# Layer 1 takes turned memories from layer 0 through DRAM, with the normalisation folded into weights and one scaling

## The chip, the cores and the metric

The kernel runs on one core of one Trainium2 chip. The time is the device time of one execution in microseconds. The engines are TensorE (PE; PEld for its weight loads), VectorE (DVE), ScalarE (ACT), GpSimd (POOL) and SyncE (SP); DMAs are issued from SP, ACT and POOL.

## The reference, cut to what matters

Two layers of a Perceiver work on latents `x` (16 batches of 64 rows of 256) and on one memory `ctx` (16 batches of 1601 rows of 256). Both layers attend to the same memory. Layer 0 attends to the raw memory with 32 chosen keys, layer 1 to its layernorm with 16 heads:

```
x = x + L0_xattn(layernorm(x), ctx, top_k=32)     # scores = q . (ctx Wk + bk), 32 largest kept
x = x + L0_attn(layernorm(x))                     # retention
x = x + L0_ffn(layernorm(x))                      # an attention over positions, then 8 experts
x = x + L1_xattn(layernorm(x), ctx, ctx)          # see below
x = x + L1_attn(layernorm(x)); x = x + L1_ffn(layernorm(x))

def L1_xattn(q, k, v):
    mu, var = mean(k), var(k)                      # over the 256 features of a memory row
    kn = (k - mu) * rsqrt(var + 1e-5) * norm_w + norm_b      # the same for v, and for q
    Q, K, V = qn @ Wq + bq, kn @ Wk + bk, kn @ Wv + bv       # 16 heads of 16
    out = softmax(0.25 * Q K^T) V + Q
    return layernorm(out, norm1_w, norm1_b) @ Wo + bo + out
```

## The kernel before

All data is fp32. A memory of 1601 rows is held with rows on the partitions as 13 chunks of 128 rows (the last of 65). To multiply it by weights or queries it has to be turned, features on the partitions: `mT`, 128 partitions by 2 halves of the features by 1601 columns. TensorE turns one 128x128 block at a time against an identity.

**Layer 0** (lines 225 to 394) works on pairs of memories, eight pairs. `turned_pair` loads two memories with SP (lines 215, 218; six buffers, so three pairs), turns them (line 248) and copies the blocks from PSUM to `mT` with ACT (line 253; two buffers, so one pair). `scored_pair` multiplies them by the queries (line 290), `choose` finds the 32 largest scores with DVE (lines 312 to 322), and `gather`, two pairs behind, turns the weights and multiplies them by the unturned memory (lines 333, 346). The turned memories are dropped after the scores.

**Retention, position attention and experts** follow (lines 515 to 896). The framework orders the instructions of each engine here by a model of its own: an instruction that is ready by that model is put ahead of program order. So work of layer 1 stands between instructions of these stages.

**Layer 1's memory attention** loads every memory again. `fetch` is `load_mem` and `normalise`: DVE takes mean and variance of each row (`bn_stats`, `bn_aggr`, lines 415 and 416), ACT a square root, DVE its reciprocal, and POOL subtracts and scales in place (line 426). `turned_mem` turns the normalised memory with TensorE (line 439) and ACT copies it out with `norm_w` and `norm_b` (line 444). `keys` (line 460, copied out by ACT at 468) and `values` (line 482, copied out by DVE at 490) multiply it by the weights `wk` and `wv`.

Memories 0 and 1 are prepared ahead of the loop (lines 899 to 909); the keys and values of memory 0 too. Then a loop runs over 128 units: 16 batches by 4 parts of the columns by 2 halves of the heads. In a unit, TensorE makes scores (981), DVE their maxima (995), ACT the exponents (997); the exponents of the unit before are turned (1010), copied out (1015, 1017) and multiplied by the values (1029). Between these, one step at a time, stand the keys and values of memory b+1, the turning of memory b+2 (`next(turns)`, eight steps in eight units) and the statistics of memory b+3 (`next(norms)`, four steps a unit from the fourth unit on). `collect` joins the parts of batch b-1 in units 1 to 3. In this loop the order of TensorE, VectorE and ScalarE is written by hand, that is, it is program order:

```python
order = {mybir.EngineType.PE, mybir.EngineType.DVE, mybir.EngineType.Activation}
with tc.manual_schedule(engines=order):
    for u in range(len(units) + 1):
```

POOL and SP keep the order of the framework's model. Weight matrices are loaded by `load_square`, here on POOL's queue.

Of the kernel before, what the change touches and what calls it, by code (L numbers as in the profile page):

```python
# [31 lines left out]
KEY_STEPS = ((1, 0), (3, 0), (3, 1), (1, 1), (2, 0), (2, 1), (0, 0), (0, 1))  # L32
TURN_STEPS = ((3, 0), (3, 1), (1, 0), (1, 1), (2, 0), (2, 1), (0, 0), (0, 1))
VALUE_STEPS = (2, 1, 1, 2, 2, 2, 2, 1)
# [31 lines left out]
def perceiver_kernel(  # L66
# [154 lines left out]
    def chunk(c):  # L221
        return P if c < 12 else TAIL


    with ExitStack() as ph:
# [11 lines left out]
        def turned_pair(k, mems, memTs):  # L237

            for h in range(2):
                mems.append(load_mem(memp, 2 * k + h))  # L240
                memTs.append(work.tile([P, 2, S], F32, name="mT", tag="mT"))
            for n0, n in SCH:
                for h in range(2):
                    for dc in range(2):
                        pt = ps_m.tile([P, 512], F32, name="pt", tag="mm")
                        for j in range((n + P - 1) // P):
                            c = n0 // P + j
                            nc.tensor.transpose(  # L248
                                pt[:, j * P : j * P + chunk(c)],
                                mems[h][0 : chunk(c), c, dc * P : (dc + 1) * P],  # L250
                                ident[0 : chunk(c), 0 : chunk(c)],
                            )
                        nc.scalar.copy(memTs[h][:, dc, n0 : n0 + n], pt[:, 0:n])  # L253
                        yield

# [143 lines left out]
    x1 = ctx.enter_context(ExitStack())  # L399
    wp = x1.enter_context(tc.tile_pool(name="x1_w", bufs=1))  # L400
# [4 lines left out]
    w_x = load_square(wp, w_x1, 4, "w_x")  # L405
    wq, wk, wv, wo = (w_x[:, i, :, :] for i in range(4))

    def normalise(mt):

        st = small.tile([P, NC, 6], F32, name="m_st", tag="m_st")  # L410
        mv = small.tile([P, NC, 2], F32, name="m_mv", tag="m_mv")
        nc.gpsimd.memset(mv[:, 12, :], 1.0)
        for c in range(NC):
            m = chunk(c)
            nc.vector.bn_stats(out=st[0:m, c, :], in_=mt[0:m, c, :])  # L415
            nc.vector.bn_aggr(out=mv[0:m, c, :], in_=st[0:m, c, :])
            yield
        sd = small.tile([P, NC], F32, name="m_sd", tag="m_sd")
        nc.scalar.activation(sd, mv[:, :, 1], AF.Sqrt, bias=eps)
        rstd = small.tile([P, NC], F32, name="m_rstd", tag="m_rstd")  # L420
        nc.vector.reciprocal(rstd, sd)
        nmean = small.tile([P, NC], F32, name="m_nmean", tag="m_nmean")
        nc.gpsimd.tensor_scalar(nmean, mv[:, :, 0], -1.0, None, ALU.mult)
        for c in range(NC):
            m = chunk(c)
            nc.gpsimd.tensor_scalar(  # L426
                mt[0:m, c, :], mt[0:m, c, :], nmean[0:m, c : c + 1], rstd[0:m, c : c + 1],
                ALU.add, ALU.mult,
            )
            yield  # L430

    def turned_mem(mt, mT, pool):

        for part, dc in TURN_STEPS:
            c0, nch, n = PARTS[part]
            pt = pool.tile([P, 512], F32, name="pt", tag="mm")
            for j in range(nch):
                c = c0 + j
                nc.tensor.transpose(  # L439
                    pt[:, j * P : j * P + chunk(c)],  # L440
                    mt[0 : chunk(c), c, dc * P : (dc + 1) * P],
                    ident[0 : chunk(c), 0 : chunk(c)],
                )
            nc.scalar.activation(  # L444
                mT[:, dc, c0 * P : c0 * P + n], pt[:, 0:n], AF.Identity,
                bias=col("L1_norm_b", dc), scale=col("L1_norm_w", dc),
            )
            yield

# [3 lines left out]
    def keys(mT, kT, pool):  # L453

        for part, oc in KEY_STEPS:
# [3 lines left out]
            for dc in range(2):  # L459
# [8 lines left out]
            nc.scalar.activation(  # L468
                kT[:, oc, n0 : n0 + n], ps[:, 0:n], AF.Identity, bias=col("L1_bk", oc)
            )  # L470
# [30 lines left out]

    mems, mTs, kvs, kvs_of = {}, {}, {}, {}

    def fetch(b):
        mems[b] = load_mem(memp, b)
        return normalise(mems[b])

    def run(steps):
        for _ in steps:
            pass  # L510

# [3 lines left out]
    with ExitStack() as ph:  # L515
# [383 lines left out]
    for b in range(2):  # L899
        run(fetch(b))  # L900
    for b in range(2):
        mTs[b] = new_mT()
        run(turned_mem(mems.pop(b), mTs[b], ps_early))
        if b == 0:
# [3 lines left out]
            run(values(mT, kvs[0][1], ps_early, nc.scalar.copy))  # L908
            run(fetch(2))
    early.close()  # L910

    with x1 as ph:
# [49 lines left out]
        project_T(ps_m, wq, qnT, head_pairs)  # L962

        bqv = act.tile([P, D], F32, name="bqv")
        nc.gpsimd.tensor_tensor(bqv, row("L1_bq"), row("L1_bv"), ALU.add)
        qnat = act.tile([P, NB, D], F32, name="qnat", tag="b")
# [130 lines left out]
        state = {}  # L1097
        joining = made_k = made_v = turns = norms = iter(())
# [396 lines left out]
```

## Time and profile before

| | us |
|---|---|
| three runs: median (lowest to highest) | 1709.47 (1709.02 to 1710.55) |
| the profiled execution, whole | 1709.81 |
| its span, first to last instruction | 1708.1 |
| PE busy in the span | 1512.6 (89%) |
| DVE, ACT, POOL busy | 1021.2 (60%), 814.6 (48%), 212.0 (12%) |
| mean granted TensorE clock | 0.954 |
| layer 0 | from the start to about 262 |
| retention, position attention, experts | about 262 to 512 |
| loop of layer 1 (first to last score, line 981) | 532.9 to 1401 |

The span and what lies around it differ by 1.7 us. A busy share is a mean over stages with different limits. In the groups of instructions, "idle before" is how long the engine had stood idle just before them, with what ended that; the busy time of matmuls counts pipelined ones side by side, so the pitch of a row of matmuls is shorter than the mean duration of one.

### The profile page before, as it was taken

Reading aid. Unit: us, or ns where it says so; the run is one execution under the profiler, and the core shown is the slowest. Engines: PE = TensorE matmul, PEld = TensorE weight load, DVE = VectorE, ACT = ScalarE, POOL = GpSimd, SP = SyncE. Lnnn points to the kernel's source line nnn. Section 1 sums busy time; section 2 is a strip of 40 time slices with the busy share of each in tenths; the row PEclk is TensorE's granted clock in tenths of the full one; section 3 lists DMA queues with packets and bytes.
Section 4 is the critical chain, followed back from the end, with each engine's and each line's share of the span. In section 5 each row is a group of like instructions: output and inputs, shape, how many; then the busy total and the mean of one; then the engine's idle time right before and its main releaser. Section 6 shows DMA issues by size and latency. Waiting matters only on the chain.

```text
span 1708.1 us, 27877 instructions
## 1 busy us (share of the span) xinstructions
PE 1512.6 (89%) x10992; PEld 1008.2 (59%) x10992; DVE 1021.2 (60%) x2197; ACT 814.6 (48%) x1984; POOL 212.0 (12%) x405
## 2 busy tenths in 40 slices
PE   4899979992939999999999999999999973889997
PEld 3555546672836666666666666666667652544455
DVE  2667847771145777677767776777766665333122
ACT  3455531350005766666667666766666551212121
POOL 0000004201010120222021202120210001000000
PEclk9999989995969999999999999999999996889999
DMA  9044203223910101110011101110100003100000
GB/s 316 1 154 138 94 19 108 83 91 97 287 58 1 40 3 41 40 41 15 29 40 41 34 11 41 40 41 3 41 2 3 3 3 122 66 1 0 0 0 25
DMA packets 76034, 92.84 MB, mean 54 GB/s; under 512 B 2408, under 2 KB 71072, under 8 KB 75776
## 3 DMA queue, kind: packets, MB, share of 16 engines
q1 hardware_dynamic: 72064, 80.85, 14.9%
q0 software_dynamic: 2688, 9.17, 1.9%
q8 instruction: 86, 1.41, 0.4%
q10 hardware_dynamic: 1152, 1.05, 0.2%
q14 instruction: 44, 0.36, 0.1%
HBM read 85.82 MB, written 5.24 MB: 53 GB/s over the span
## 4 chain that ended last, share of the span: by engine, by line
PE 72%; ACT 10%; DVE 9%; issue 4%; DMA 3%; SPq 1%; POOL 0%; ACTq 0%; DVEq 0%; POOLq 0%
PE ps_v L482 10%; PE ps_k L460 7%; ACT a L997 6%; PE sc L981 6%; PE po L1029 6%; PE pt L1010 5%; PE ps_h L1334 5%; PE ps_p L183 3%; PE ps_o L1352 3%; PE pt L248 3%; PE sc L290 3%; PE pu L346 3%; PE pt L439 2%; PE ps_n L197 2%; DVE nmax L995 2%
## 5 line engine op out<-in xcount | busy, mean ns | idle before, releaser
L997 ACT ACTIVATE a<-sc,nmax 128x384 f32<-128x384 f32 (+2 forms) x512 | 300.3, 596 | 170.8 <-DVE nmax L995 170.5
L995 DVE TENSOR_REDUCE nmax<-sc 128x1 f32<-128x384 f32 (+2 forms) x512 | 258.2, 567 | 109.8 <-PE sc L981 109.7
L482 PE MATMUL ps_v<-w_x,mT 128*128 128x256 f32 (+1 forms) x832 | 205.3, 385 | 22.3 <-ACT kT L468 22.3
L1010 PEld LDWEIGHTS pt<-ident,a 128*128 128x128 f32 (+1 forms) x1664 | 189.3, 141 | 52.1 <-issue 28.2
L1017 DVE COPY aT<-pt 128x512 f32<-128x512 f32 (+1 forms) x288 | 191.0, 685 | 37.8 <-PE pt L1010 30.8
L1010 PE MATMUL pt<-ident,a 128*128 128x128 f32 (+1 forms) x1664 | 207.5, 274 | 2.3 <-ACT kT L468 0.7
L460 PE MATMUL ps_k<-mT,w_x 128*128 128x384 f32 (+2 forms) x512 | 207.9, 528 | 0.1
L482 PEld LDWEIGHTS ps_v<-w_x,mT 128*128 128x128 f32 (+1 forms) x832 | 144.7, 186 | 49.6 <-ACT kT L468 31.3
L460 PEld LDWEIGHTS ps_k<-mT,w_x 128*128 128x128 f32 x512 | 87.4, 190 | 108.1 <-issue 77.6
L1029 PE MATMUL po<-aT,v 128*32 128x128 f32 (+1 forms) x3328 | 119.1, 277 | 10.9 <-DVE aT L1017 7.0
L444 ACT ACTIVATE mT<-pt,cols 128x384 f32<-128x384 f32 (+2 forms) x128 | 87.1, 684 | 79.0 <-PE pt L439 76.3
L981 PE MATMUL sc<-kT,qh 32*128 32x384 f32 (+2 forms) x1024 | 123.1, 548 | 0.0
L426 POOL TENSOR_SCALAR memt<-memt,m_nmean,m_rstd 128x256 f32<-128x256 f32 (+1 forms) x208 | 112.2, 557 | 7.3 <-PE po L1029 4.3
L997 ACT ACTIVATION_READ_ACCUMULATOR a<-sc,nmax 128x1 f32 x512 | 105.1, 205 | 0.0
L1029 PEld LDWEIGHTS po<-aT,v 128*32 128x32 f32 (+1 forms) x3328 | 82.7, 109 | 35.5 <-issue 13.5
L490 DVE COPY v<-ps_v 128x512 f32<-128x512 f32 (+1 forms) x120 | 69.2, 576 | 49.3 <-PE po L1029 30.7
L415 DVE BATCH_NORM_STATS2 m_st<-memt 128x6 f32<-128x256 f32 (+1 forms) x208 | 82.6, 401 | 3.4 <-DMA memt<-in_mem_dram 3.0
L1334 PE MATMUL ps_h<-xnT,fw 128*128 128x512 f32 x192 | 84.1, 596 | 0.0
L253 ACT COPY mT<-pt 128x512 f32<-128x512 f32 (+1 forms) x128 | 58.0, 503 | 53.3 <-PE pt L248 52.6
L248 PE MATMUL pt<-ident,memt 128*128 128x128 f32 (+1 forms) x416 | 63.2, 292 | 22.8 <-DMA memt<-in_mem_dram 21.6
L468 ACT ACTIVATE kT<-ps_k,cols 128x384 f32<-128x384 f32 (+2 forms) x128 | 76.0, 593 | 13.2 <-PE ps_k L460 13.2
L1015 ACT COPY aT<-pt 128x512 f32<-128x512 f32 x128 | 76.9, 601 | 0.7 <-PE pt L1010 0.7
(310 smaller groups left out, 1945.8 us busy)
## 6 DMA issues: line engine op xcount, KB each, us to landing
memt<-in_mem_dram SPq DMA_DIRECT2D x32, 1536.0 KB, 9.1
w<-in_moe_w_dram SPq DMA_DIRECT2D x16, 1024.0 KB, 5.1
fw<-in_fff_w_dram SPq DMA_DIRECT2D x6, 1024.0 KB, 12.8
memt<-in_mem_dram SPq DMA_DIRECT2D x32, 65.0 KB
w_x<-in_w_x_dram POOLq DMA_DIRECT2D x2, 1024.0 KB, 12.2
rows<-in_rows_dram POOLq DMA_DIRECT2D x1, 1430.5 KB, 9.9
X<-in_x_dram SPq DMA_DIRECT2D x1, 1024.0 KB
w_mha<-in_w_mha_dram POOLq DMA_DIRECT2D x1, 1024.0 KB
```

The costliest lines, as they stand in the source:

```text
L248: nc.tensor.transpose(pt[:, j * P : j * P + chunk(c)], mems[h][0 : chunk(c), c, dc * P : (dc + 1) * P], ident[0 : chunk(c), 0 : chunk(c)],)
L426: nc.gpsimd.tensor_scalar(mt[0:m, c, :], mt[0:m, c, :], nmean[0:m, c : c + 1], rstd[0:m, c : c + 1], ALU.add, ALU.mult,)
L444: nc.scalar.activation(mT[:, dc, c0 * P : c0 * P + n], pt[:, 0:n], AF.Identity, bias=col("L1_norm_b", dc), scale=col("L1_norm_w", dc),)
L460: nc.tensor.matmul(ps[:, 0:n], lhsT=wk[:, dc, oc * P : (oc + 1) * P], rhs=mT[:, dc, n0 : n0 + n], start=(dc == 0), stop=(dc == 1),)
L482: nc.tensor.matmul(ps[0 : chunk(c), j, :], lhsT=mT[:, dc, c * P : c * P + chunk(c)], rhs=wv[:, dc, :], start=(dc == 0), stop=(dc == 1),)
L981: nc.tensor.matmul(scs[j][:, 0:n], lhsT=qh[rs, oc, b, :, :], rhs=kT[rs, oc, c0 * P : c0 * P + n], start=True, stop=True,)
L995: nc.vector.reduce_max(out=nm, in_=sc[:, 0:n], axis=AX.X, negate=True)
L997: nc.scalar.activation(aj[:, 0:n], sc[:, 0:n], AF.Exp, bias=nm, accum_out=tot[:, blk, part : part + 1])
L1010: nc.tensor.transpose(pt[0:m, j * P : (j + 1) * P], a[j][:, c * P : c * P + m], ident)
L1017: nc.vector.tensor_copy(aT[0:m, :], pt[0:m, :])
L1029: nc.tensor.matmul(po[32 * j : 32 * j + 32, :], lhsT=v[0:m, c0 + c, blk * 32 : (blk + 1) * 32], rhs=aTs[c][0:m, j * P : (j + 1) * P], star ...
L1334: nc.tensor.matmul(ps, lhsT=fw1[:, f, dc, m * P : (m + 1) * P], rhs=xnT[:, dc, cs], start=(dc == 0), stop=(dc == 1),)
```

## The change

Layer 0 keeps the turned memories. After each stretch of columns is copied to `mT`, ACT issues a store of it to a DRAM tensor `turned_d[b]`: four stores for a memory, 64 in all. They are the raw memory, not the normalised one.

Layer 1 loads `turned_d[b]` into `mT` instead of turning the memory again. The normalisation is taken apart. The mean over the features and `norm_w` go into the weights `wk` and `wv` once (scaled rows, from which the column mean is subtracted), `norm_b` goes into the bias of the keys (`kbias`) and into `bqv`. The reciprocal deviation of each memory row is a factor of a column of `mT`: `deviations` takes the variances with the same `bn_stats` and `bn_aggr`, computes the reciprocal root with 18 small POOL instructions in place of ACT's square root, and stores 1664 numbers to DRAM from POOL's queue; `scaled_mem` loads them back onto all 128 partitions (`rb`), loads `mT`, and multiplies with eight POOL instructions.

The deviations of memories 0, 1 and 2 are computed in layer 0 from its own loads, so layer 1 loads 13 unturned memories instead of 16; its buffers for them go from two to one. In the loop the loads of `rb` and `mT` are written at the start of a batch, the scalings two a unit in units 3 to 6, the statistics three steps a unit. `load_square` moves from POOL's queue to SP's.

```diff
 def load_square(pool, src, n, name):
-        nc.gpsimd.dma_start(
+        nc.sync.dma_start(
...
+    def deviations(b, mt):
...
+        nc.gpsimd.memset(mv[:, 12, :], 1.0)
+        for c in range(NC):
+            nc.vector.bn_stats(out=st[0:m, c, :], in_=mt[0:m, c, :])
+            nc.vector.bn_aggr(out=mv[0:m, c, :], in_=st[0:m, c, :])
+            yield
...
+        nc.gpsimd.tensor_scalar(var, mv[:, :, 1], EPS, None, ALU.add)
...
+        nc.gpsimd.tensor_scalar(
+            bits, var.bitcast(I32), -0.5, float(0x5F3759DF), ALU.mult, ALU.add
+        )
...
+        for _ in range(4):
+            nc.gpsimd.tensor_tensor(sq, rs, rs, ALU.mult)
+            nc.gpsimd.tensor_tensor(sq, sq, var, ALU.mult)
+            nc.gpsimd.tensor_scalar(sq, sq, -0.5, 1.5, ALU.mult, ALU.add)
+            nc.gpsimd.tensor_tensor(rs, rs, sq, ALU.mult)
+        nc.gpsimd.dma_start(out=rstd_d[b].rearrange("(c p) -> p c", p=P), in_=rs)
+        yield
...
                         nc.scalar.copy(memTs[h][:, dc, n0 : n0 + n], pt[:, 0:n])
+                        if dc == 1:
+                            nc.scalar.dma_start(
+                                out=turned_d[2 * k + h][:, :, n0 : n0 + n],
+                                in_=memTs[h][:, :, n0 : n0 + n],
+                            )
...
+        for b in range(2):
+            run(deviations(b, first_mems[b]))
...
+                    if k == 1:
+                        run(deviations(2, mems[0]))
...
-    memp = x1.enter_context(tc.tile_pool(name="x1_mem", bufs=2))
+    memp = x1.enter_context(tc.tile_pool(name="x1_mem", bufs=1))
...
-    def normalise(mt):
...
-    def turned_mem(mt, mT, pool):
...
+    def scaled_mem(b, mT):
+        rb = memp.tile([P, S], F32, name="rb", tag="rb", bufs=2)
+        nc.sync.dma_start(out=rb, in_=rstd_d[b][0:S].partition_broadcast(P))
+        nc.sync.dma_start(out=mT, in_=turned_d[b])
+        yield
+        for c0, _, n in PARTS:
+            for dc in range(2):
+                sl = slice(c0 * P, c0 * P + n)
+                nc.gpsimd.tensor_tensor(mT[:, dc, sl], mT[:, dc, sl], rb[:, sl], ALU.mult)
+                yield
...
+    for wi in (wk, wv):
+        for c in range(2):
+            nc.gpsimd.tensor_scalar(wi[:, c, :], wi[:, c, :], col("L1_norm_w", c), None, ALU.mult)
+        ps = ps_early.tile([P, D], F32, name="ps_wm", tag="mm")
+        for c in range(2):
+            nc.tensor.matmul(ps, lhsT=mean, rhs=wi[:, c, :], start=(c == 0), stop=(c == 1))
+        for c in range(2):
+            nc.vector.tensor_tensor(wi[:, c, :], wi[:, c, :], ps, ALU.subtract)
...
     for b in range(2):
-        run(fetch(b))
-    for b in range(2):
         mTs[b] = new_mT()
-        run(turned_mem(mems.pop(b), mTs[b], ps_early))
+        run(scaled_mem(b, mTs[b]))
         if b == 0:
...
-            run(fetch(2))
...
                     if b + 2 < B:
                         mTs[b + 2] = new_mT()
-                        turns = turned_mem(mems.pop(b + 2), mTs[b + 2], ps_m)
+                        scaling = scaled_mem(b + 2, mTs[b + 2])
+                        next(scaling)
                     if b + 3 < B:
-                        norms = fetch(b + 3)
+                        norms = deviations(b + 3, load_mem(memp, b + 3))
...
                 if u % 8 >= 3:
-                    for _ in range(4):
+                    for _ in range(3):
                         next(norms, None)
-                if u % 8 == 7:
-                    run(norms)
-                next(turns, None)
+                if u % 8 in (3, 4, 5, 6):
+                    for _ in range(2):
+                        next(scaling, None)
```

More of the change, by code (lines that the diff above doesn't have):

```diff
@@ L32 @@
 KEY_STEPS = ((1, 0), (3, 0), (3, 1), (1, 1), (2, 0), (2, 1), (0, 0), (0, 1))
-TURN_STEPS = ((3, 0), (3, 1), (1, 0), (1, 1), (2, 0), (2, 1), (0, 0), (0, 1))
 VALUE_STEPS = (2, 1, 1, 2, 2, 2, 2, 1)
@@ L90, in perceiver_kernel @@
     small = ctx.enter_context(tc.tile_pool(name="small", bufs=3))
+    kept = ctx.enter_context(tc.tile_pool(name="kept", bufs=1, space=bass.MemoryType.DRAM))
+    turned_d = [kept.tile([P, 2, S], F32, name=f"turned{b}", tag=f"turned{b}") for b in range(B)]
+    rstd_d = [kept.tile([NC * P], F32, name=f"rstd{b}", tag=f"rstd{b}") for b in range(B)]
     def load_square(pool, src, n, name):
         t = pool.tile([P, n, 2, D], F32, name=name, tag=name)
-        nc.gpsimd.dma_start(
+        nc.sync.dma_start(
             out=t.rearrange("p n c o -> p (n c) o"),
@@ L222, in chunk, with run @@
         return P if c < 12 else TAIL
+    def deviations(b, mt):
+        st = small.tile([P, NC, 6], F32, name="m_st", tag="m_st")
+        mv = small.tile([P, NC, 2], F32, name="m_mv", tag="m_mv")
+        nc.gpsimd.memset(mv[:, 12, :], 1.0)
+        for c in range(NC):
+            m = chunk(c)
+            nc.vector.bn_stats(out=st[0:m, c, :], in_=mt[0:m, c, :])
+            nc.vector.bn_aggr(out=mv[0:m, c, :], in_=st[0:m, c, :])
+            yield
+        var = small.tile([P, NC], F32, name="m_var", tag="m_var")
+        nc.gpsimd.tensor_scalar(var, mv[:, :, 1], EPS, None, ALU.add)
+        rs = small.tile([P, NC], F32, name="m_rs", tag="m_rs")
+        bits = rs.bitcast(I32)
+        nc.gpsimd.tensor_scalar(
+            bits, var.bitcast(I32), -0.5, float(0x5F3759DF), ALU.mult, ALU.add
+        )
+        sq = small.tile([P, NC], F32, name="m_sq", tag="m_sq")
+        for _ in range(4):
[5 more added lines that the diff above has]
+        yield
+    def run(steps):
+        for _ in steps:
+            pass
     with ExitStack() as ph:
@@ L399, in perceiver_kernel @@
     x1 = ctx.enter_context(ExitStack())
-    wp = x1.enter_context(tc.tile_pool(name="x1_w", bufs=1))
-    memp = x1.enter_context(tc.tile_pool(name="x1_mem", bufs=2))
+    x1_wp = x1.enter_context(tc.tile_pool(name="x1_w", bufs=1))
+    memp = x1.enter_context(tc.tile_pool(name="x1_mem", bufs=1))
     kvp = x1.enter_context(tc.tile_pool(name="x1_kv", bufs=2))
@@ L404, in perceiver_kernel @@
     ps_early = early.enter_context(tc.tile_pool(name="x1_ps_e", bufs=2, space=PSUM))
-    w_x = load_square(wp, w_x1, 4, "w_x")
+    w_x = load_square(x1_wp, w_x1, 4, "w_x")
     wq, wk, wv, wo = (w_x[:, i, :, :] for i in range(4))
-    def normalise(mt):
[L410 to L430, printed above, removed]
@@ L432, in turned_mem @@
-    def turned_mem(mt, mT, pool):
[L434 to L448, printed above, removed]
+    def scaled_mem(b, mT):
[8 more added lines that the diff above has]
+                yield
@@ L468, in keys @@
             nc.scalar.activation(
-                kT[:, oc, n0 : n0 + n], ps[:, 0:n], AF.Identity, bias=col("L1_bk", oc)
+                kT[:, oc, n0 : n0 + n], ps[:, 0:n], AF.Identity, bias=kbias[:, oc : oc + 1]
             )
@@ L500, in new_kv @@
         )
[L502 to L510, printed above, removed]
+    mTs, kvs, kvs_of = {}, {}, {}
     kvs_of[0] = x1.enter_context(tc.tile_pool(name="x1_kv0", bufs=1))
@@ L588, in perceiver_kernel @@
             nc.vector.tensor_tensor(X[:, k, :], X[:, k, :], ps, ALU.add)
+    mean = x1_wp.tile([P, P], F32, name="mean")
+    nc.gpsimd.memset(mean, 1.0 / D)
+    nb = x1_wp.tile([P, 2, P], F32, name="nb")
+    for c in range(2):
+        nc.gpsimd.tensor_scalar(nb[:, c, :], ones, col("L1_norm_b", c), None, ALU.mult)
+    kbias = x1_wp.tile([P, 2], F32, name="kbias")
+    ps = ps_early.tile([P, 2], F32, name="ps_kb", tag="mm")
+    for oc in range(2):
+        for c in range(2):
+            nc.tensor.matmul(
+                ps[:, oc : oc + 1], lhsT=wk[:, c, oc * P : (oc + 1) * P],
+                rhs=col("L1_norm_b", c), start=(c == 0), stop=(c == 1),
+            )
+    at = COLS["L1_bk"][0]
+    nc.vector.tensor_tensor(kbias, ps, cols[:, at : at + 2], ALU.add)
+    bqv = x1_wp.tile([P, D], F32, name="bqv")
+    nc.gpsimd.tensor_tensor(bqv, row("L1_bq"), row("L1_bv"), ALU.add)
+    ps = ps_early.tile([P, D], F32, name="ps_vb", tag="mm")
+    for c in range(2):
+        nc.tensor.matmul(ps, lhsT=nb[:, c, :], rhs=wv[:, c, :], start=(c == 0), stop=(c == 1))
+    nc.vector.tensor_tensor(bqv, bqv, ps, ALU.add)
+    for wi in (wk, wv):
+        for c in range(2):
+            nc.gpsimd.tensor_scalar(wi[:, c, :], wi[:, c, :], col("L1_norm_w", c), None, ALU.mult)
+        ps = ps_early.tile([P, D], F32, name="ps_wm", tag="mm")
+        for c in range(2):
+            nc.tensor.matmul(ps, lhsT=mean, rhs=wi[:, c, :], start=(c == 0), stop=(c == 1))
+        for c in range(2):
+            nc.vector.tensor_tensor(wi[:, c, :], wi[:, c, :], ps, ALU.subtract)
     with ExitStack() as ph:
@@ L962, in perceiver_kernel @@
         project_T(ps_m, wq, qnT, head_pairs)
-        bqv = act.tile([P, D], F32, name="bqv")
-        nc.gpsimd.tensor_tensor(bqv, row("L1_bq"), row("L1_bv"), ALU.add)
         qnat = act.tile([P, NB, D], F32, name="qnat", tag="b")
@@ L1097, in perceiver_kernel @@
         state = {}
-        joining = made_k = made_v = turns = norms = iter(())
+        joining = made_k = made_v = scaling = norms = iter(())
         a = None
```

## The prediction

> **What bounds the kernel now.** I read the chain of waits first, then the groups of instructions, then the loop of layer 1 batch by batch.
>
> ```profile
> PE 72%; ACT 10%; DVE 9%; issue 4%; DMA 3%; SPq 1%; POOL 0%; ACTq 0%; DVEq 0%; POOLq 0%
> L439 PE MATMUL pt<-ident,memt 128*128 128x128 f32 x384 | 65.1, 276 | 5.2 <-ACT aT L1015 3.3 <-ACT mT L444 1.6 <-ACT v L490 0.2
> L444 ACT ACTIVATE mT<-pt,cols 128x384 f32<-128x384 f32 (+2 forms) x128 | 87.1, 684 | 79.0 <-PE pt L439 76.3
> L415 DVE BATCH_NORM_STATS2 m_st<-memt 128x6 f32<-128x256 f32 (+1 forms) x208 | 82.6, 401 | 3.4 <-DMA memt<-in_mem_dram 3.0
> L426 POOL TENSOR_SCALAR memt<-memt,m_nmean,m_rstd 128x256 f32<-128x256 f32 (+1 forms) x208 | 112.2, 557 | 7.3 <-PE po L1029 4.3
> ```
>
> TensorE sets the end. ACT's 87 us and POOL's 112 us are off the path. TensorE's 416 turnings look like 72 us by busy time, but matmuls are pipelined: runs of them advance by about 0.11 us each.
>
> The loop has its own measure of what the turning costs. Statistics run for memory b+3, turning for b+2; so batch 13 has no statistics, and batch 14 neither. I cut the time at the first score of a batch (columns: length, then busy of PE, PEld, DVE, ACT, POOL, clock, DMA share, GB/s):
>
> ```profile
> 640.30:696.50 56.20, 53.91 (x500) 37.88 (x497) 41.02 (x93) 37.64 (x101) 11.17 (x23) 1.00 0.11 32
> 1258.20:1312.20 54.00, 53.29 (x500) 37.81 (x496) 35.00 (x66) 35.10 (x98) 4.12 (x8) 1.00 0.02 3
> 1312.20:1363.30 51.10, 50.38 (x472) 34.69 (x468) 35.00 (x66) 29.78 (x90) 3.72 (x7) 1.00 0.02 3
> 729.41 1.99 PE L482 MATMUL ps_v<-w_x,mT 128*128 128x256 f32 x8 [1.40 <-ACT kT L468]
> ```
>
> A batch with both takes 56.2 us, without statistics 54.0, without turning 51.1. So the turning is worth 2.9 us a batch, the statistics 2.2: about 0.7 in the last unit, where ACT changes its table for the square root and back, and 1.5 to 1.7 in unit 4 (counted from 0), where four `bn` pairs delay the maxima, the exponents and then TensorE (last line).
>
> **The loop of layer 1.** Turning and root go; 13 `bn` pairs (401 + 178 ns each, lines 415 and 416) stay, three to a unit. In batch 14 DVE stands idle some 0.8 us before the maxima and 1.0 before the copy of the values in units 5 to 7, which hides three pairs (1.74 us). After unit 3, which also holds `collect`, it has none: 1.5 us remain. A batch is 51.1 + 1.5 = 52.6. Batches 1 to 12: 12 x 3.6 = 43; batch 13: 2.9; batch 0, which shows no statistics stall now: 2.9. Together -49. Bounds: no stall at all, 12 x 5.1 + 5.8 = -67; statistics as dear as now, 51.1 + 2.2 = 53.3, 12 x 2.9 + 5.8 = -41.
>
> POOL's scaling: rows for two-input instructions are
>
> ```profile
> L734 POOL TENSOR_TENSOR X<-X,rows 128x2048 f32<-128x2048 f32 x1 | 5.3, 5311 | 4.9 <-DVE xa L154 4.9
> L1076 POOL TENSOR_TENSOR both<-parts 128x256 f32<-128x256 f32 x16 | 11.6, 727 | 213.0 <-DVE parts L1068 213.0
> ```
>
> or 2.56 ns an element and 0.07 us each: 2 x 1601 elements in eight instructions are 8.8 us a batch, in place of 13 x 0.557 = 7.2. The keys of that memory come a batch later, so I take nothing. "GPSIMD Engine Reference", section 3.1, of the Trainium skill speaks against such work there: it gives 4497 ns for 2048 elements, about twice VectorE's time; this trace has 5311, and either is hidden.
>
> **Layer 0, its steady pairs.** A pair's period, loads on SP, and the first blocks that TensorE turns of them:
>
> ```profile
> 138.10:161.50 23.40, 22.70 (x155) 12.70 (x153) 17.19 (x16) 12.65 (x26) 0.00 (x0) 1.00 0.45 141
> 138.25 0.37 SPq L215 DMA_DIRECT2D memt<-in_mem_dram  x1
> 139.57 0.40 SPq L215 DMA_DIRECT2D memt<-in_mem_dram  x1
> 146.41 0.66 PE L248 MATMUL pt<-ident,memt 128*128 128x128 f32 x4
> 151.82 0.66 PE L248 MATMUL pt<-ident,memt 128*128 128x128 f32 x4
> ```
>
> TensorE is full and the DMA engines 0.45 busy with 3.3 MB. The stores add as many bytes: 0.9. And the loads are just in time: they are issued when `gather` frees the buffers, the first landing about 7.4 us later (145.7, used at 146.4), the second 10.9 (150.4, used at 151.8). Some 1.6 MB of stores fall between 138 and 145; at 141/0.45 = 313 GB/s they are 5 us of traffic. Sharing half and half, the first load is late by about 2.6 us, the second by no more beyond that. I take 2.8 us for each of the five pairs whose loads wait for buffers (issued at 91, 115, 138, 162, 185): +14. Bounds 0 (slack holds) and 5 x 5 = 25. "DMA: Bandwidth & Descriptors", section "Issuing engines are not separate DMA queues", of the Trainium skill speaks against queues of their own: all DMAs share the same engines and interleave. With truly separate queues this term would be 0 and the sum 14 lower.
>
> ACT issues 64 stores:
>
> ```profile
> L879 ACTq DMA_DIRECT2D done<-ye x8: 326/326/344, 430.1 to 485.0; - x8
> L879 ACTq EVENT_SEMAPHORE  x4: 17/17/17, 429.7 to 484.6; - x4
> ```
>
> 64 x 0.33 = 21 us, in gaps of ACT (12.65 of 23.4 busy) but between copies that TensorE waits for: I take +3, bounds 0 and 10.
>
> **Layer 0, its start.** The second line above is a wait ahead of the store. In the trace's operands the DMAs of SP and ACT name eight semaphores in turn, and each waits for the one eight places back. At the start:
>
> ```profile
> 17.35 0.37 SPq L215 DMA_DIRECT2D memt<-in_mem_dram  x1
> 22.33 0.37 SPq L215 DMA_DIRECT2D memt<-in_mem_dram  x1
> 23.51 7.56 PE L248 MATMUL pt<-ident,memt 128*128 128x128 f32 x41 [2.92 <-DMA memt<-in_mem_dram]
> 24.66 0.59 ACT L253 COPY mT<-pt 128x512 f32<-128x512 f32 x1 [3.44 <-PE pt L248]
> 28.93 3.49 ACT L253 COPY mT<-pt 128x512 f32<-128x512 f32 x9 [0.27 <-PE pt L248]
> ```
>
> SP issues 15 loads at once (the weights now second to the latents), which land one memory per 4.6 to 5 us: 18.5, 23.5, 28, 33, 38, 43. The first pair's eight stores come after them in order, so store 1 waits for memory 2 (28 in place of 21), 3 for memory 3, 5 for memory 4, 7 for memory 5, each later still by the stores' own bytes (2.6 MB, 6 us): 43 + 6 = 49. ACT waits in order, behind it the copies that free TensorE's PSUM, then the query's. Its copies end near 49.5 instead of 32.4: +17, all on the path, for the queries' products follow and only then the first scores. Bounds: 0, if the stores stand ahead of the later loads; 20. The 39 `bn` pairs of memories 0 to 2 (22.6 us of DVE) lie in DVE's idle stretch before the first scores (2 tenths busy): nothing, or up to 5 if they push into `choose`.
>
> **Between.** 52 turnings and 39 `bn` pairs go out of the stages before the loop. The turnings ran at 295 to 301 and 373 to 379, where DVE's layernorms were the wait, so they gave nothing; 20 us of keys and values of memory 0 stand in a stretch where TensorE is full (327 to 365) and may move forward into those gaps: -5. Against it, the weights' preparation (about 1.5 us of TensorE, 2.5 of DVE, 4 of POOL) waits for `w_x`, which lands some 6 us after it is freed at 261, next to retention's products: +5. I take 0.
>
> **The sum.** 1709.8 (the profiled execution; its span is 1.7 lower, the median 0.3 lower) - 49 + 14 + 3 + 17 + 0 = **1695**.
>
> **The rivals.** *No wait at the start* (the framework puts stores ahead of later loads): 1695 - 17 = 1678. For it: the order is the model's and can't be read from this trace. Against: SP's buffers are free, so a model issues all loads at once. *The loads of `rb` stand first on SP* (slower than before). `rb` waits for the reciprocals: the last `bn` about 2.5 us before a batch ends, 18 POOL instructions of 0.26 us, the issue (0.9) and a store of 1664 four-byte pieces, nearest row `by_head` with 2.7 us for 1024 pieces: 6 us into the batch. If `mT` (1.6 MB) and the next memory (1.6) queue behind it, with 0.8 for `rb` they land 12 to 15 us later, at 18 to 21, and DVE's first `bn` comes at 25. A store of 10 us or more turns that into a DVE stall, which TensorE sees in full: 3 us x 13 batches is +39, less what is left of the gain: 1725 to 1730. It decides from 1.2 us a batch. For it: program order. Against: the next memory's buffer is free before `rb` is ready. *Gain and costs cancel:* layer 0 at its upper bounds gives 1695 + 3 + 11 + 7 = 1716, loop at its lower 1703.
>
> **How the numbers follow.** The sum as it stands, 1683 to 1706: 0.47. No start wait: 0.23. Cancelled within 0.2% (about what a measurement of this kernel can tell from no change): 0.08. Slower, by `rb` (0.11) or by DMA contention in layer 0 (0.11): 0.22. So faster 0.70, same 0.08, slower 0.22. The range 1668 to 1728 leaves out a tenth on either side.
>
> **What would show it.** A batch of the loop near 52.6 us, unit 4 the longest; no waits of `bn` for a load. In layer 0 the first score near 68 instead of 51.3, ACT idle on a DMA between copies at 21 to 49; periods of 26 us with TensorE waiting for loads; a DMA share near 0.9. I am wrong if a loop batch keeps 55 us or more, or if the first score stays at 51.

## The result and the profile after

The changed kernel takes 1916.7 us (1915.2 to 1918.3) against 1709.8 in the same comparison: 1.121 times as long, interval 1.119 to 1.123. That is far outside the forecast of 1668 to 1728. By the profiled executions (spans 1708.1 and 1913.7) the 206 us lie so:

| stage | before | after | forecast | found |
|---|---|---|---|---|
| start to the first score of layer 0 | 51.3 | 60.1 | +17 | +9 |
| first score of layer 0 to the end of its last | 165.3 | 201.3 | +17 | +36 |
| layer 0's end (260.5, 305.5) to the loop's first score | 272.5 | 280.5 | 0 | +8 |
| loop, first score to the first of the last unit | 868.0 | 1022.8 | -49 | +155 |
| behind the loop | 307 | 305 | 0 | -2 |

So the loop is the miss. First the chain of waits and the groups of instructions of the changed kernel (a group: busy, mean ns of one, then idle time before it and its releaser):

```profile
PE 50%; DMA 14%; issue 14%; POOL 10%; DVE 8%; ACT 4%; SPq 0%; POOLq 0%; ACTq 0%; DVEq 0%
...
L1043 PE MATMUL pt<-ident,a 128*128 128x128 f32 (+1 forms) x1664 | 225.6, 285 | 177.9 <-ACT pos L1069 170.2
...
L461 POOL TENSOR_TENSOR mT<-mT,rb 128x384 f32<-128x384 f32 (+2 forms) x128 | 127.2, 1024 | 246.6 <-DMA rb<-rstd 191.1
...
L235 DVE BATCH_NORM_STATS2 m_st<-memt 128x6 f32<-128x256 f32 (+1 forms) x208 | 83.5, 402 | 9.0 <-DMA memt<-in_mem_dram 8.7
```

TensorE's share of the chain falls from 72 to 50%; DMA and GpSimd, 3 and 0% before, hold 24. TensorE now stands 170 us ahead of line 1043, waiting for ScalarE. VectorE's statistics wait for no load (the 8.7 us are one wait at the start), so the stall that my rival expected on VectorE isn't there. By the windows, a batch with statistics, then unit 2 of the next one (counted from 0), then batch 14 without statistics (columns as in the prediction):

```profile
633.70:702.30 68.60, 52.99 (x472) 36.34 (x468) 40.83 (x92) 29.38 (x89) 16.80 (x36) 0.90 0.21 62
715.63:738.00 22.37, 8.76 (x76) 6.29 (x72) 5.31 (x13) 3.54 (x12) 8.35 (x10) 0.69 0.35 111
1519.40:1570.40 51.00, 50.53 (x476) 34.74 (x472) 34.93 (x66) 29.58 (x89) 3.72 (x7) 1.00 0.02 3
```

TensorE has no more work than was forecast (472 matmul records, as many as in the prediction's batch without turning; 53 us busy), but unit 2 takes 22.4 us where its neighbours take 6.6. Without that stall a batch with statistics (68.3 us, mean of 12) would take 68.3 - 15.9 = 52.4 us; 52.6 was forecast. A batch of 55 us or more is also the sign of being wrong that the prediction named. The timeline of the batch that starts at 702.3, one engine after the other, shows who waits (start, duration, engine, line; idle time and releaser in brackets):

```profile
707.64 1.22 POOL L252 DMA_DIRECT2D rstd<-m_rs  x1 [0.29 <-POOL m_rs L251]
...
716.74 0.33 SPq L455 DMA_DIRECT2D rb<-rstd  x1
...
723.31 7.89 POOL L461 TENSOR_TENSOR mT<-mT,rb 128x512 f32<-128x512 f32 x8 [14.45 <-DMA rb<-rstd]
731.18 0.23 POOL L1082 TENSOR_TENSOR wt<-low,nmax 128x32 f32<-128x32 f32 x1
...
731.44 0.23 ACT L1083 ACTIVATE wt<-wt 128x32 f32<-128x32 f32 x1 [16.87 <-POOL wt L1082]
...
731.88 1.11 PE L1043 MATMUL pt<-ident,a 128*128 128x128 f32 x4 [13.17 <-ACT pos L1069]
```

The store of 1664 pieces takes 9.1 us from issue until `rb` can be asked for, `rb` 6.6 more, the eight scalings 7.9. All that time a subtraction of 32 numbers a partition, `wt` of `collect`, stands behind them on GpSimd; ScalarE's exponent of it is due at 714.6, and on ScalarE's queue the copy (`pos`) that TensorE waits for stands behind that. In the kernel before, `wt` ran as soon as VectorE had its minima, 12.5 us into a batch (the one from 640.3), and ScalarE hardly waited for it. The lines are `wt` in that batch, all of ScalarE's waits for it (us in all, times, longest), and the same waits in the changed kernel:

```profile
652.84 0.24 POOL L1049 TENSOR_TENSOR wt<-low,nmax 128x32 f32<-128x32 f32 x1 [12.19 <-DVE low L1047]
...
ACT wt L1050 <- POOL wt L1049: 4.4, 14, 0.8
...
ACT wt L1083 <- POOL wt L1082: 219.5, 15, 17.3
```

In program order `wt` stands ahead of the scalings: it is written into unit 1, they into units 3 to 6. But GpSimd's order is the framework's, and in the trace all eight scalings come first. (Program order on GpSimd was not tried.)

### The profile page after: what moved, and what is told of

It reads as the page before. It is cut to its first block, busy times and chain, and to the rows that moved or that the text cites. A ratio compares the mean times of both kernels' runs of the same rounds, so it can differ in the third digit from the quotient of the medians.

```text
span 1913.7 us, 27343 instructions
## 1 busy us (share of the span) xinstructions
PE 1525.3 (80%) x10596; PEld 996.0 (52%) x10596; DVE 1022.1 (53%) x2187; ACT 694.8 (36%) x1814; POOL 306.4 (16%) x615
## 3 DMA queue, kind: packets, MB, share of 16 engines
q1 hardware_dynamic: 76214, 119.73, 19.6%
## 4 chain that ended last, share of the span: by engine, by line
PE 50%; DMA 14%; issue 14%; POOL 10%; DVE 8%; ACT 4%; SPq 0%; POOLq 0%; ACTq 0%; DVEq 0%
DMA rstd<-m_rs 5%; PE ps_v L496 5%; POOL mT L461 5%; PE ps_h L1368 4%; DMA rb<-rstd 4%; PE ps_k L474 4%; PE pt L1043 4%; PE ps_p L187 3%; PE ps_o L1386 3%; PE sc L332 3%; PE pu L388 3%; PE sc L1014 2%; PE po L1062 2%; ACT a L1030 2%; PE ps_n L201 2%
## 5 line engine op out<-in xcount | busy, mean ns | idle before, releaser
L1043 PE MATMUL pt<-ident,a 128*128 128x128 f32 (+1 forms) x1664 | 225.6, 285 | 177.9 <-ACT pos L1069 170.2
L1043 PEld LDWEIGHTS pt<-ident,a 128*128 128x128 f32 (+1 forms) x1664 | 197.7, 146 | 236.3 <-ACT pos L1069 173.3
L496 PE MATMUL ps_v<-w_x,mT 128*128 128x256 f32 (+1 forms) x832 | 215.9, 400 | 14.4 <-ACT kT L482 14.4
L496 PEld LDWEIGHTS ps_v<-w_x,mT 128*128 128x128 f32 (+1 forms) x832 | 152.4, 195 | 40.2 <-ACT kT L482 20.3
L461 POOL TENSOR_TENSOR mT<-mT,rb 128x384 f32<-128x384 f32 (+2 forms) x128 | 127.2, 1024 | 246.6 <-DMA rb<-rstd 191.1
L1062 PE MATMUL po<-aT,v 128*32 128x128 f32 (+1 forms) x3328 | 120.2, 278 | 13.4 <-ACT aT L1048 6.9
L1069 ACT COPY pos<-po 128x128 f32<-128x128 f32 x128 | 33.8, 264 | 174.3 <-PE po L1062 174.3
L482 ACT ACTIVATE kT<-ps_k,kbias 128x384 f32<-128x384 f32 (+2 forms) x128 | 76.2, 595 | 27.6 <-PE ps_k L474 27.6
```

Source lines behind the costliest of these rows:

```text
L461: nc.gpsimd.tensor_tensor(mT[:, dc, sl], mT[:, dc, sl], rb[:, sl], ALU.mult)
L482: nc.scalar.activation(kT[:, oc, n0 : n0 + n], ps[:, 0:n], AF.Identity, bias=kbias[:, oc : oc + 1])
L496: nc.tensor.matmul(ps[0 : chunk(c), j, :], lhsT=mT[:, dc, c * P : c * P + chunk(c)], rhs=wv[:, dc, :], start=(dc == 0), stop=(dc == 1),)
L1043: nc.tensor.transpose(pt[0:m, j * P : (j + 1) * P], a[j][:, c * P : c * P + m], ident)
L1062: nc.tensor.matmul(po[32 * j : 32 * j + 32, :], lhsT=v[0:m, c0 + c, blk * 32 : (blk + 1) * 32], rhs=aTs[c][0:m, j * P : (j + 1) * P], star ...
```

## The experiments: the loop

**The place of `wt`.**

```diff
-            nc.gpsimd.tensor_tensor(wt, low.unsqueeze(2).to_broadcast(wide), nmax, ALU.subtract)
+            nc.vector.tensor_tensor(wt, low.unsqueeze(2).to_broadcast(wide), nmax, ALU.subtract)
...
-            nc.gpsimd.tensor_tensor(tot, tot, wt, ALU.mult)
+            nc.vector.tensor_tensor(tot, tot, wt, ALU.mult)
```

> Two small operations of collect (the weights wt and the totals tot, 32 numbers a partition) run on VectorE in place of GpSimd; all else is as in the changed kernel. Theory A (GpSimd's order): the stall of 15.9 us in a batch's third unit exists only because wt stands behind the eight scalings in GpSimd's queue, and these wait for rb. It goes: third unit 6.5 to 7 us in place of 22.4, a batch 52.5 to 53.5 in place of 68.3, whole time 1917 - 13 x 15.5 = about 1715 (1705 to 1725). Rival B (the loads behind rb on SyncE are late, and VectorE's statistics wait): the stall moves to VectorE's bn and stays near its size, the time stays above 1890.

Measured: 1715.3 us, ratio 1.0029 (1.0017 to 1.0042). Unit 2 takes 6.5 us, a batch 52.4. The window of a batch:

```profile
646.60:699.00 52.40, 50.73 (x472) 34.76 (x468) 41.08 (x95) 29.58 (x89) 16.41 (x34) 1.00 0.26 81
```

And a line of this kernel's waits in the loop (us in all, times, longest):

```profile
POOL mT L461 <- DMA rb<-rstd: 178.3, 12, 15.2
```

The scalings wait for `rb` about as long as before the edit (178 us in all, 186 in the changed kernel's loop), but TensorE and ScalarE no longer wait behind them. Two tiny instructions moved off GpSimd are worth 201 us. Theory A holds, rival B falls.

**Deviations a batch ahead.**

```diff
                     if k == 1:
                         run(deviations(2, mems[0]))
+                        run(deviations(3, mems[1]))
...
-                    if b + 3 < B:
-                        norms = deviations(b + 3, load_mem(memp, b + 3))
+                    if b + 4 < B:
+                        norms = deviations(b + 4, load_mem(memp, b + 4))
```

> The loop computes the deviations of memory b+4 in place of b+3 (layer 0 those of memory 3 too), so the load of rb finds them stored a whole batch ago. Theory A: the scalings then wait only for the loads of mT and rb, issued at the batch's start, some 7 us; with 8 us of scalings wt comes 15 to 16 us into the batch where it is due at about 13: 2 to 4 us of the stall stay, a batch 54 to 57, whole time 1735 to 1760. Rival D (the loads of mT are themselves the late ones): 8 us or more of the stall stay, above 1810.

Measured: 1721.9 us, ratio 1.0063 (1.0042 to 1.0083); batches of 52.5 to 53.4. That is below the expected 1735 to 1760: the scalings start some 7 us into the batch, and `wt` comes 14 to 15 us into it instead of 12, which costs little (unit 2: 6.6 to 7.5 us). So the stall needs both: `wt` behind the scalings, and scalings that wait long. The 6.6 us above `wt_dve` lie ahead of the loop (layer 0's first score at 70.9 in place of 63.9).

**A shorter chain**, in three attempts. First, statistics a unit earlier:

```diff
-                    for _ in range(3):
+                    for _ in range(4):
                         next(norms, None)
```

> The statistics run four steps a unit from the fourth unit on, not three, so they end one unit (5.6 us) earlier, and the deviations are stored that much earlier. Theory A: the chain from the last statistics over store, load of rb and scalings to wt ends 5.6 us earlier: stall 15.9 to about 10.3, less 0 to 0.7 for dearer statistics, whole time 1917 - 13 x 5 = about 1850 (1840 to 1860). Rival C (the store takes its 20 us by competing with the other loads, not by its place): the stall stays within 2 us of 15.9, the time above 1890.

Measured: 1914.6 us, unit 2 at 19.6 to 22.2. A miss: by the time rival C comes true, but the queues show another reason than its own. SyncE's queue and GpSimd in the batch that starts at 710.9:

```profile
703.87 0.38 SPq L219 DMA_DIRECT2D memt<-in_mem_dram  x1
719.29 0.33 SPq L455 DMA_DIRECT2D rb<-rstd  x1
719.67 0.40 SPq L222 DMA_DIRECT2D memt<-in_mem_dram  x1
720.16 0.33 SPq L456 DMA_DIRECT2D mT<-turned  x1
...
731.23 7.90 POOL L461 TENSOR_TENSOR mT<-mT,rb 128x512 f32<-128x512 f32 x8 [20.27 <-DMA mT<-turned]
```

`rb` is indeed asked for earlier: 8.4 us into the batch in place of 14.4. But the framework now put the load of `mT` behind it, where the changed kernel has it ahead; so 1.6 MB are asked for only when the store has landed, and arrive 11 us later. I tried to turn that order round by writing the load of `mT` first (on top of `stats_early`):

```diff
-        nc.sync.dma_start(out=rb, in_=rstd_d[b][0:S].partition_broadcast(P))
         nc.sync.dma_start(out=mT, in_=turned_d[b])
+        nc.sync.dma_start(out=rb, in_=rstd_d[b][0:S].partition_broadcast(P))
```

> As stats_early (statistics done a unit earlier, wt still on GpSimd), but the load of mT is written ahead of that of rb, so SyncE's order is mT, next memory, rb, where stats_early had next memory, rb, mT and let the load of mT stand behind the wait of rb. Theory A: the scalings then wait for rb alone, which comes 5 to 6 us earlier than in the changed kernel: third unit 16 to 18 us in place of 22.4, whole time 1840 to 1865. Rival C (an earlier end of the statistics is worth nothing): third unit at 21 or more, 1900 or above.

Measured: 1917.8 us, unit 2 at 21 to 22 (once 19.5). This tested nothing: SyncE's queue still ran next memory, `rb`, `mT` (699.1, 714.5, 715.4), since that order is the model's and not the program's. The third attempt, also on top of `stats_early`, takes `rb` off SyncE:

```diff
-        nc.sync.dma_start(out=rb, in_=rstd_d[b][0:S].partition_broadcast(P))
+        nc.gpsimd.dma_start(out=rb, in_=rstd_d[b][0:S].partition_broadcast(P))
```

> As stats_early, but the load of rb goes from SyncE's queue to GpSimd's, straight behind the store that it waits for. SyncE then waits for no deviation, and the load of mT stands behind no wait. Theory A (the stall in the third unit ends when store, load of rb and eight scalings are through, counted from the last statistics; in stats_early and early_swap the load of mT, issued behind rb, took back what was won): scalings start about 15.5 us into the batch in place of 21, third unit 16 to 18.5 us in place of 22.4, whole time 1840 to 1870. Rival C (the end of the statistics plays no part): third unit at 21 or more, 1900 or above.

Measured: 1881.4 us, ratio 1.1006 (1.0988 to 1.1023), unit 2 at 18.0 to 19.1 us (once 21.2). GpSimd and ScalarE in the batch that starts at 706.5:

```profile
705.34 1.24 POOL L252 DMA_DIRECT2D rstd<-m_rs  x1 [0.29 <-POOL m_rs L251]
718.69 0.59 POOL L455 DMA_DIRECT2D rb<-rstd  x1 [12.11 <-DMA mT<-turned]
724.11 7.90 POOL L461 TENSOR_TENSOR mT<-mT,rb 128x512 f32<-128x512 f32 x8 [4.83 <-issue]
...
732.24 0.23 ACT L1083 ACTIVATE wt<-wt 128x32 f32<-128x32 f32 x1 [13.49 <-POOL wt L1082]
```

The stall follows the chain: ScalarE waits 13.5 us in place of 16.9, and the loop is 41 us shorter (the whole time 35, since layer 0 ended 7 us later in these runs' profile). It is less than expected (1840 to 1870) because the store became slower: it is issued 6.5 us earlier in the batch, but `rb` can be asked for 13.4 us after that, where the batch of the changed kernel shows 9.1. The store now runs beside two loads of 1.6 MB; that these slow it is likely, but was not tried by itself.

## The experiments: layer 0

**The stores alone**, in the kernel before (the `dma_start` of the change's `turned_pair`, nothing that reads it):

> The kernel before, with only the 64 stores of layer 0 from ScalarE added; nothing reads them. Theory F: they cost what layer 0 grew by without the deviations: pairs of 28 to 31 us, +35 in all, and the first score within 3 us of 51.3 if the scattered stores of deviations caused the late start; whole time 1709 + 36 = 1745 (1738 to 1755). My prediction's step (ScalarE waits for stores at the start because of the semaphores it shares with SyncE): the first score at 58 or later, the time at 1755 or above.

Measured: 1753.8 us, ratio 1.0260 (1.0242 to 1.0278). First score 55.3, last 256.5 against 216.6: the stores are 40 of the 45 us that layer 0 grew by. The first score lies between the two expectations, +4 by the stores alone; the other 5 us come only with the deviations, by a way that no run separates. (In five kernels whose layer 0 is written alike it lies between 57.5 and 63.9.) ScalarE at the start of the changed kernel:

```profile
21.10 0.57 ACTq L290 DMA_DIRECT2D turned<-mT  x1
...
30.53 0.70 ACT L288 COPY mT<-pt 128x512 f32<-128x512 f32 x2
34.02 0.52 ACTq L290 DMA_DIRECT2D turned<-mT  x1
34.58 0.33 ACT L288 COPY mT<-pt 128x65 f32<-128x65 f32 x2 [3.35 <-DMA turned<-mT]
...
38.66 0.52 ACTq L290 DMA_DIRECT2D turned<-mT  x1
39.22 0.59 ACT L136 COPY xnT<-ps_t 128x512 f32<-128x512 f32 x1 [2.63 <-DMA turned<-mT]
```

The first store goes out as soon as its copies are done. The sixth and the eighth wait, by the releasers each for an earlier store, and the copies stand behind them. The timeline of a steady pair (ScalarE, then TensorE) shows what happens later:

```profile
229.34 0.52 ACTq L290 DMA_DIRECT2D turned<-mT  x1
231.47 1.60 ACT L340 ACTIVATE sco<-sc,qbk 128x1601 f32<-128x1601 f32 x1 [2.17 <-PE sc L332]
235.86 0.59 ACT L288 COPY mT<-pt 128x512 f32<-128x512 f32 x1 [2.78 <-DMA turned<-mT]
...
236.50 1.12 PE L375 MATMUL pt<-ident,pr 128*128 128x128 f32 x4 [4.14 <-ACT mT L288]
```

The window of this pair:

```profile
206.80:237.50 30.70, 25.85 (x152) 14.33 (x151) 17.20 (x17) 13.25 (x25) 0.00 (x0) 0.89 0.62 214
```

The last stores of the two memories are issued at 228.0 and 229.3. The next pair's first copy goes into the first memory's `mT` buffer and has to wait until that has been read, at about 235.8, and TensorE stands 4.1 us behind that copy. Then it runs slower for a while: four turnings take 1.12 us where they take 0.66 elsewhere, and the pair's granted clock is 0.89.

**The issuing queue.**

```diff
-                            nc.scalar.dma_start(
+                            nc.gpsimd.dma_start(
                                 out=turned_d[2 * k + h][:, :, n0 : n0 + n],
```

> Layer 0's 64 stores are issued from GpSimd's queue in place of ScalarE's; the loop is as in the changed kernel. Theory E (the issues, 0.52 us each, take ScalarE's time between copies): a pair falls from 28 to 31 us to about 24, layer 0 by about 35 us, whole time about 1880. Rival F (the copies of the next pair wait for the stores to have read the two mT buffers): a pair stays at 27 or more, the time at 1900 or above, and the wait of the first copy of a pair for a store is seen.

Measured: 1917.8 us; first score 50.4, last 260.9. The issues are not what the pairs cost, as rival F has it. But the start's delay is gone, and later pairs give it back.

**A third buffer.**

```diff
-                memTs.append(work.tile([P, 2, S], F32, name="mT", tag="mT"))
+                memTs.append(work.tile([P, 2, S], F32, name="mT", tag="mT", bufs=3))
```

> The kernel with wt and tot on VectorE (wt_dve), and three mT buffers in layer 0 in place of two. Theory F (the first copy of a pair waits for the last pair's stores to have read the two buffers, 3 to 4 us, and TensorE runs at a lower clock after that idle time): a pair falls from about 30 us to 24 to 26, the wait of mT's copy for a store nearly goes, layer 0 by about 30 us, whole time 1715 - 30 = 1685 (1672 to 1697). Rival G (the stores' bytes hold up the loads): a pair stays at 28 or more, the time above 1705.

Measured: 1702.1 us, ratio 0.9952 (0.9937 to 0.9967), 13 below `wt_dve` and not 30. The wait of the steady pairs' copies for a store is gone, but pairs take 25 to 28 us (the last 33), and TensorE now waits for loads. Theory F is about half of it. For the rest, one run halves the bytes at the same number of issues (partitions 0 to 63 alone, in the kernel before), another the issues at the same bytes:

> The kernel before with three mT buffers in layer 0 and 64 stores from ScalarE of half the bytes (partitions 0 to 63 alone); nothing reads them. The issues are as many as before. Theory G (the stores' bytes delay the loads): a pair 25 or less where wt_buf3 had 27, whole time 1724 or less. Rival L (ScalarE's issues): a pair stays at 27, whole time 1732 to 1738.

> As buf3_fast, but each memory is stored in two pieces (columns 0 to 1023 and 1024 to 1600) in place of four: half the issues on ScalarE, the same bytes. Theory L (with three buffers the rest of a pair's 27 us over 23.4 comes from ScalarE's issues of 0.52 us between copies): a pair 25 to 26, 8 to 12 us below buf3_fast. Rival G (it comes from loads that share the DMA engines with the stores): a pair stays at 27, within 4 us of buf3_fast.

Measured: half the bytes, 1726.6 us in one run, pairs of 24.6 to 25.5; half the issues, 1712.1 us, pairs of 26 to 35, 12 us slower than four stores a memory (`buf3_fast`, below), which neither theory had forecast and no run explains. The window of a pair of `wt_buf3`, with all the bytes:

```profile
147.50:174.50 27.00, 23.58 (x152) 13.04 (x151) 17.16 (x17) 12.88 (x26) 0.00 (x0) 1.00 0.70 245
```

And of `stores_half3`, with half of them:

```profile
135.10:160.10 25.00, 23.47 (x154) 13.07 (x152) 17.15 (x17) 12.87 (x26) 0.00 (x0) 1.00 0.69 203
```

TensorE is busy alike; half of the bytes are worth 2.0 us, where a pair with all of them takes 3.6 more than the 23.4 of before. So the bytes may well be all of the rest (rival G's reason); L falls. With the stores on GpSimd as well:

> As wt_buf3, and the 64 stores are issued from GpSimd's queue. Theory H (ScalarE's issues and its waits at the start cost about 10 us at the start and 1 us a pair): first score of layer 0 near 51 in place of 57 to 71, whole time 10 to 20 below wt_buf3. Rival I (GpSimd issues a store in 1.2 us and later than ScalarE, so buffers come free later): as wt_buf3 within 4 us, or slower.

Measured: 1706.3 us, ratio 0.9985 (0.9972 to 0.9997): first score at 50.3, but pairs of 29 to 31, TensorE waiting 32 us for loads. Both halves of that expectation came true, at different places.

**The store of the deviations in long pieces** (on top of `wt_dve`):

```diff
-        nc.gpsimd.dma_start(out=rstd_d[b].rearrange("(c p) -> p c", p=P), in_=rs)
+        yield
+        pt = pool.tile([P, 512], F32, name="pt", tag="mm")
+        nc.tensor.transpose(pt[0:NC, 0:P], rs, ident)
+        rt = small.tile([NC, P], F32, name="m_rt", tag="m_rt", bufs=1)
+        nc.vector.tensor_copy(rt, pt[0:NC, 0:P])
+        nc.gpsimd.dma_start(out=rstd_d[b].rearrange("(c p) -> c p", p=P), in_=rt)
...
```

> As wt_dve, but TensorE turns the 128x13 deviations, VectorE copies them to 13x128, and the store writes 13 pieces of 512 bytes in place of 1664 of 4; in the loop these steps and the loads of rb and mT stand in the second unit of the next batch. Theory J (the scattered stores of layer 0's start occupy the DMA engines, which show a share near 1.0 at 40 to 70 us while they move 80 to 130 GB/s): the share there falls to under 0.6, the first score comes at 50 to 56 in place of 57 to 71, whole time 5 to 15 below 1715. Rival K (they only take long, at no cost to others): start as in wt_dve, within 4 us of 1715.

Measured: 1710.3 us, ratio 1.0007 (0.9996 to 1.0018), 5 below `wt_dve`. The windows from 40 to 60 us of the changed kernel (last two columns: DMA share, GB/s):

```profile
40.00:50.00 10.00, 10.00 (x20) 4.35 (x19) 0.37 (x2) 2.75 (x4) 7.55 (x27) 0.80 0.95 104
50.00:60.00 10.00, 10.00 (x45) 6.94 (x43) 1.39 (x2) 1.17 (x2) 0.27 (x1) 0.88 1.27 83
```

And of `wt_fast`:

```profile
40.00:50.00 10.00, 10.00 (x21) 4.19 (x21) 0.00 (x0) 3.04 (x5) 3.73 (x19) 0.85 0.98 310
50.00:60.00 10.00, 10.00 (x50) 6.07 (x50) 1.80 (x4) 0.89 (x2) 0.62 (x1) 1.00 0.00 0
```

Theory J holds for the DMA engines: while three scattered stores ran, they showed busy for some 20 us and little data moved. It doesn't hold for the first score (58.4), which is ScalarE's matter (`buf3_fast_first`, below). The store in long pieces lands 2.1 us after its issue (median of 16).

## The experiments: between, and a version that beats both

> As buf3_fast, without the scaling of wk and wv by norm_w and without the subtraction of their column means (the keys and values are those of unscaled weights). Theory N: the turning of xa starts about 39 us after the end of layer 0 in place of 43.4, whole time 3 to 6 below buf3_fast. Rival (the 8 us come from GpSimd's scaling of memories 0 and 1): 43 still, within 2 us of buf3_fast.

Measured: one run, 1697.0 us; from layer 0's end to the turning of `xa` 39.4 us in place of 43.4 (38.7 before), to the loop's first score 276.0 in place of 280.2 in `buf3_fast`. So, by this run, the preparation of the weights is half of the 8 us. VectorE in the changed kernel, with the layernorm's statistics queued behind:

```profile
344.25 0.75 DVE L627 TENSOR_TENSOR w_x<-w_x,ps_wm 128x256 f32<-128x256 f32 x2 [1.43 <-PE ps_wm L625]
346.05 0.75 DVE L627 TENSOR_TENSOR w_x<-w_x,ps_wm 128x256 f32<-128x256 f32 x2 [1.04 <-PE ps_wm L625]
```

The other half (the gate's products take 8.0 us in place of 4.8) I leave open.

> wt_dve with both single gains: three mT buffers in layer 0 (wt_buf3, 1702) and the deviations stored as 13 pieces of 512 bytes (wt_fast, 5 us below wt_dve). Theory: the two touch different stages and add: 1702 - 5 = 1697 (1692 to 1702), faster than the kernel before by 0.5 to 1.0%. Rival: the start's gain only moves the wait into layer 0's loads, and the time stays at 1702 or above.

Measured: 1700.0 us, ratio 0.9943 (0.9930 to 0.9957): inside the theory's range, though the gains add to 2 us and not to 5. The next version adds one edit to it:

```diff
-                            nc.scalar.dma_start(
+                            (nc.gpsimd if k == 0 else nc.scalar).dma_start(
                                 out=turned_d[2 * k + h][:, :, n0 : n0 + n],
```

> As buf3_fast, but the first pair's eight stores are issued by GpSimd, the later ones by ScalarE as before. Theory M (at the start ScalarE's copies stand behind stores that wait, and TensorE then runs at a lower clock; in store_pool and wt_buf3_pool the first score came at 50): first score at 50 to 52 in place of 58, whole time 5 to 8 below buf3_fast, 1692 to 1696. Rival: the loads of pairs 3 and 4 set the pace by then, and the gain is below 2 us.

Measured: **1692.8 us, ratio 0.9901 (0.9886 to 0.9916)**, first score at 49.5. This version (`wt` on VectorE, three `mT` buffers, deviations in long pieces, the first pair's stores from GpSimd) beats both kernels, the one before by 1.0%.

> As buf3_fast_first, with the preparation of the weights (the block from mean to the subtraction from wk and wv) written behind the experts, just ahead of the keys of memory 0, in place of ahead of the position attention. Theory N (in the changed kernel the layernorm ahead of the position attention waits behind this block on VectorE, 4.7 us, and the gate's weights behind it on GpSimd, 3 us): from the end of layer 0 to the first score of the loop 272 to 276 us in place of 280, whole time 4 to 8 below buf3_fast_first. Rival: the framework puts ready instructions ahead anyway, and keys of memory 0 come later into a stretch without cover: no gain, or some us lost.

Measured: 1695.2 us, no gain. The layernorm of `xa` did come 5 us earlier (38.2). It was given back on GpSimd, where the eight scalings of a memory now fell between the indirect DMAs of the experts' dispatch (the turning of the dispatched rows came at 171.8 us after layer 0's end, at 166.5 without this edit; the loop's first score at 286.0 in place of 280.3):

```profile
444.27 0.97 POOL L854 DMA_INDIRECT disp<-y,to_row  x1 [1.71 <-DMA disp<-y,to_row]
445.27 1.27 POOL L466 TENSOR_TENSOR mT<-mT,rb 128x512 f32<-128x512 f32 x1
446.95 1.01 POOL L854 DMA_INDIRECT disp<-y,to_row  x1 [0.42 <-DMA disp<-y,to_row]
448.00 5.86 POOL L466 TENSOR_TENSOR mT<-mT,rb 128x512 f32<-128x512 f32 x6
454.01 1.01 POOL L854 DMA_INDIRECT disp<-y,to_row  x1 [0.16 <-issue]
```

## Why the prediction was wrong, and where it was right

- **The step that failed** is "The keys of that memory come a batch later, so I take nothing", on GpSimd's scaling. I priced the scalings (8.8 us; 7.9 measured) and asked when their result is needed. I did not ask what stands behind them on GpSimd's queue while they wait, as I did for ScalarE's stores. The list was short: `wt`, `tot`, the sums of `collect`, and the group of line 1076 stood in my own fence. What the runs showed in its place: `wt` stands behind the waiting scalings, and TensorE behind `wt`, for 15.8 us in each of 13 batches. That is 205 us; the loop lies 204 off the forecast (+155 against -49), and moving `wt` gives 201 back.
- **The rival on `rb`** had the right transfer and the wrong victim. It put `rb` at 6 us into the batch (5.8 by its terms); it was asked for at 14.4. Of the 8.6 us, the store's landing is 5.2 (7.9 against 2.7 by the row of `by_head`), the last statistics 2.3 later than taken, GpSimd's 18 instructions and the issue 1.2. A row of 64-byte pieces is no price for 4-byte pieces. Its engine, VectorE, waited for no load, and its price (+39) was a fifth.
- **The loop's gain** was right: 50 us in `wt_dve` against 49, with unit 4 the longest (7.64 us), as named.
- **Layer 0's start**: half of the mechanism held. ScalarE does wait at stores (3.3 and 2.6 us), and with the first pair's stores on GpSimd the first score comes at 49.5 to 50.8. But it waits for its own earlier stores, not for memories 2 to 5. The first store went out at 21.1 without a wait, so stores did go ahead of later loads, which is the condition of the rival *No wait at the start*. My premise that SyncE issues all loads at once does not fit my own rows, two loads 5 us apart (17.35 and 22.33). So the eight stores were through at 39 us and not at 49, and the start cost +9 in place of +17. Part of the delay is the clock, 0.84 at 20 to 60 us where before has 1.00.
- **Layer 0's pairs**: forecast +2.8 by late loads, found +4 to +7. The late loads are real and about that size (+3.6 with a third buffer, +1.6 with half the bytes). What I missed is that a store reads the buffer that it leaves from, so two `mT` buffers no longer suffice. `wt_buf3` is worth 13 us. The issues, which I put at 0.33 us and +3 in all, take 0.52 us each, but `store_pool` shows no gain from taking them off ScalarE.
- **Between**: forecast 0 out of -5 and +5, found +8. The weights' preparation is some 4 us (`noprep`); that the expected gain did not come was not followed up.
- **"DMA: Bandwidth & Descriptors"**, section "Rules for kernel authors", of the Trainium skill says that a strided last dimension is lowered to one descriptor per element and should be rearranged to be contiguous. No run here counts descriptors; that the rearrangement pays, they show: 20.3 us to landing in the changed kernel (the one store whose landing its trace holds), 2.1 us for the same 1664 numbers in pieces of 512 bytes.

## What to carry to other kernels

Where an engine is given an instruction that waits for a DMA, list what comes behind it on that engine until the wait ends, however small: the smallest of them can hold up the kernel. Take that list from the queue's order in a trace, not from the program. A store adds a reader to its buffer, so the count of buffers has to be looked at again. Where a framework orders a queue, an edit that makes one transfer early can put another behind it; read the queue's order in the new trace before reading the time.

## What the hardware showed that I had not expected

The cost of these DMAs went by their pieces: 6.5 KB in 1664 pieces of 4 bytes took 9 to 20 us, in 13 pieces of 512 bytes 2.1. While the scattered ones ran, the DMA engines showed busy (share 0.95 to 1.27) at 83 to 104 GB/s, where memory loads show 0.98 at 310.

In layer 0 of the changed kernel TensorE waits five times for more than 3 us for a copy that waits for a store. After waits of 4.1, 4.1 and 4.7 us the next four turnings took 1.1 us, after 3.2 and 3.5 us the usual 0.66, so a wait of 4 us cost more than its length:

```profile
148.05 0.66 PE L375 MATMUL pt<-ident,pr 128*128 128x128 f32 x4 [3.17 <-ACT mT L288]
...
236.50 1.12 PE L375 MATMUL pt<-ident,pr 128*128 128x128 f32 x4 [4.14 <-ACT mT L288]
```
